# Issuing the stores of GpSimd-made rows two to four turns later, and the memory scan's transposes of h one turn later, in a two-layer attention and mixture-of-experts network on one core

## Chip, cores and metric

One NeuronCore of a Trainium2 chip (trn2) runs the whole program in one launch. The metric is the device time of one execution in microseconds (us). Before the change, three executions took 3901.26, 3905.21 and 3909.09 us; the median is 3905.21 us.

## What is computed

The input is x of shape 16 x 512 x 128 in fp32: 16 sequences of 512 tokens. Two layers follow each other, each with an attention part and a feed-forward part that read the same normalised input:

```python
x = L0_attn_x
xn = _layernorm(x, axis=-1)
x = x + _L0_attn_ref(xn, ...) + _L0_ffn_ref(xn, ...)
xn = _layernorm(x, axis=-1)
x = x + _L1_attn_ref(xn, ...) + _L1_ffn_ref(xn, ...)
```

- `_L0_attn_ref` is a small memory network, trained while it reads. The tokens are cut into 8 chunks of 64; for each chunk, in order, a two-layer perceptron (128 to 256 to 128, `h = silu(k @ w0.T)`, `y = h @ w1.T`, then an RMS norm) gets one clipped gradient step with momentum. This is the **scan**: 8 steps, each needs the weights that the step before it left. Afterwards every token is read through the final weights: the **readout**.
- `_L0_ffn_ref` is a convolution over time, full attention with 16 heads of 8, a layernorm, then 8 dense experts (128 to 512 to 128) weighted by a softmax gate, and a second layernorm.
- `_L1_attn_ref` is causal attention, a convolution of its context, a second causal attention with the convolved queries, and a projection.
- `_L1_ffn_ref` sends each token to its best 8 of 32 experts, with at most 128 tokens per expert.

## The kernel before, in words

**Turns.** The program is unrolled Python. Each piece of work on one sequence b is a generator that emits some instructions and then yields. A loop (`Turns.run`) steps every live generator once per *turn*: those with number 0 first (`tops`: scores and their row maxima), then 1 (`back`: scores again, exponentials, weighted values), then the rest. A stage is entered at a turn that is written into a table (`b * TA + 60` for `post0`, `t0 + b * TBB` for `middle`), or waits for a mark that another stage sets (`after`, `mark`). `idle(n)` yields n times and emits nothing.

**What a turn fixes.** TensorE's instructions run in exactly the order in which the turns emit them (`manual_schedule(engines=ORDERED)`, and ORDERED holds TensorE alone). On the other engines, and on SyncE's queue that issues nearly all transfers, a scheduler orders the instructions when the program is built; the place at which an instruction is emitted is its priority there. Once built, each queue is worked off strictly in its order: an instruction that waits for a semaphore holds up all that stand behind it.

**Filling.** A turn holds about 2.75 us of TensorE work by the kernel's own estimate (TURN). `ffn(b)`, the dense experts of layer 0, runs as a filler: per turn it emits as many of its 64 half-units as the credit left by the other stages allows. Where the turn has too little work for TensorE and no `ffn` work was emitted lately, `fill` adds one matmul whose result nobody reads.

**The stages, in order of time.** Turns 0 to 32 normalise x and load constants. From turn 32 to turn 486 the scan (8 steps, then 16 readouts, one begun every 6 turns) runs beside layer-0 attention (`front0`, `tops`, `back`, `post0`, one sequence each 32 turns) and `ffn`. From turn 480 on layer 1 follows at one sequence each 44 turns: `middle`, `front1`, `tops` and `back` for the first attention, `between`, `tops` and `back` for the second, `last`. Each of the 64 causal `tops` holds the lock "p1" for 11 turns, so 44 turns are exactly what four of them take. From turn 1165 the routed experts (`moe`) run beside the last three sequences; the last `last(15)` marks turn 1272, and the stages `total(b)` write the output.

**Stores of rows that GpSimd makes.** Four stages end a row of work on GpSimd and store it to device memory through SyncE:
- `post0(b)`, L1116: x1, after a layernorm whose last instruction is GpSimd's add at L237, to x1d. Then come four idle turns, then the transpose of x1 and its store at L1121, and the mark "x1", for which `ffn(b)` waits. x1d[0] is read back by `ffn` at L530 and, once `ffn` has rewritten it, by `middle` at L1163.
- `readout(b)`, L1034: y, after GpSimd's L1031 to L1033, to acc. It is the readout's last instruction. The tile y shares its buffer (tag h or ds, one buffer each) with the hTq of the readout two later.
- `middle(b)`, L1170: x2, after a layernorm and GpSimd's add at L1169, to acc. Then come three idle turns and the next layernorm.
- `last(b)`, L1279: x2, after GpSimd's add at L1278, to acc (for the 13 sequences that finish before the routed experts' counts are known).

Behind such a store on SyncE's queue stand, among others: the loads of the score operands kx and qx (L364), the little store of the row maxima and their two loads back (`top<-m` at L412, `qx<-top` at L416), the scan's token load xc (L778), and the experts' weights ew (L512, L516).

**The scan step.** `timed` starts each part at a turn counted from the step's start: `hidden(q)` for q = 0..3 at turns 1 to 4 (two pairs of matmuls into pp, two ACT instructions for the sigmoid sg, and one turn later VectorE's product h at L851 and three GpSimd instructions for the derivative ds at L853 to L855); `hidden_turned(q, i)` at turns 4 to 7 (four TensorE transposes of h, and the ACT copy to hT at L861); `gradient(0)` at 7 and `gradient(1)` at 9 (eight pairs of matmuls py from hT, then a chain over ACT, VectorE and GpSimd). The step goes on when all parts are through. `project(c + 2)` of the scan loads the tokens of a later chunk and makes its keys on GpSimd (L802 to L806).

Of the kernel before, what the change touches and what calls it, by code (L numbers as in the profile page):

```python
# [82 lines left out]
def network(ctx: ExitStack, tc: tile.TileContext, a, out):  # L83
# [85 lines left out]
    def drop():  # L169

        read[0] += 1
# [7 lines left out]
    def flat(ap):  # L179
        return ap.rearrange("p t d -> p (t d)")  # L180
# [84 lines left out]
    def idle(n):  # L265
        for _ in range(n):
            yield
# [494 lines left out]
    def scan(s1):  # L762
# [47 lines left out]
        def step(c):  # L810
# [47 lines left out]
            def hidden_turned(q, i):  # L858
                yield from room()
                tp = turn4(lambda t: h[:, 4 * q + t, i * P : (i + 1) * P])  # L860
                nc.scalar.copy(hT[q][:, i, :], tp)  # L861
                yield
# [49 lines left out]
            def back(q):  # L912
# [10 lines left out]
            yield from timed(  # L923
                (0, before()), (0, turned(kT, lambda t: k[:, t, :], 0)), (1, turned(kT, lambda t: k[:, 4 + t, :], 1)),
                *[(1 + q, hidden(q)) for q in range(4)],
                *[(4 + 2 * q + i, hidden_turned(q, i)) for q in range(2) for i in range(2)],
                (7, gradient(0)), (9, gradient(1)),
            )
            dyT = s1.tile([P, NT * P], F32, tag="kT", name="dyT")
            yield from timed(  # L930
# [58 lines left out]
        def readout(b):  # L989
            xb = s1.tile([P, TB, D], F32, tag=("k", "v")[b % 2], bufs=2, name="xb")  # L990
            nc.sync.dma_start(xb, x_b[b])
            xT = s1.tile([P, S], F32, tag=("hT0", "kT")[b % 2], name="xTr")
            nc.sync.dma_start(xT, xt[0, b])
            yield from idle(2)
            q = s1.tile([P, TB, D], F32, tag=("yh", "eb", "gy")[b % 3], name="rq")
            yield from silu_half(flat(q), lambda t: xT[:, t * P : (t + 1) * P], A("wq"))
            rq = sm.tile([P, TB], F32, tag="r_q", name="r_q")
            rms_rows(rq, q, TB, s1)
            nc.gpsimd.tensor_tensor(q, q, bc(row["qn"], 1, TB), ALU.mult)
            nc.gpsimd.tensor_tensor(q, q, bc(rq, 2, D), ALU.mult)  # L1000
            yield from idle(5)
            yield from room()
            qT = s1.tile([P, S], F32, tag="sg", bufs=2, name="qT")
            transpose_tokens(qT, q)
            yield from idle(1)
            hT = s1.tile([P, 2, S], F32, tag=("h", "ds")[b % 2], name="hTq")

            def hidden(i):
                yield from room()
                pp = hold("ppq")  # L1010
                mm(pp, w0T[:, i * P : (i + 1) * P], qT)
                nc.scalar.activation(hT[:, i, :], pp, AF.Tanh, scale=0.5)
                nc.scalar.activation(hT[:, i, :], hT[:, i, :], AF.Copy, scale=0.5, bias=0.5)
                yield
                nc.vector.tensor_tensor(hT[:, i, :], hT[:, i, :], pp, ALU.mult)
                drop()
                yield

            yield from side(hidden(0), hidden(1))
            yield from room()  # L1020
            py = toks(work("pyq"))
            for t in range(TB):
                for i in range(2):
                    mm(py[:, t, :], hT[:, i, t * P : (t + 1) * P], w1T[:, i, :], start=(i == 0), stop=(i == 1))
            ry = sm.tile([P, TB], F32, tag="r_yq", name="r_yq")
            y = s1.tile([P, TB, D], F32, tag=("h", "ds")[b % 2], name="yq")
            nc.scalar.copy(y, py)
            rms_rows(ry, y, TB, s1)
            yield from idle(3)
            nc.vector.tensor_tensor(y, y, bc(ry, 2, D), ALU.mult)  # L1030
            nc.gpsimd.tensor_tensor(y, y, bc(ln, 1, TB), ALU.mult)  # L1031
            nc.gpsimd.tensor_tensor(y, y, q, ALU.add)
            nc.gpsimd.tensor_tensor(y, y, xb, ALU.add)  # L1033
            nc.sync.dma_start(acc_b[b], y)  # L1034
            yield

# [58 lines left out]
    def post0(b):  # L1095
        yield from after(("back", 0, b, 0, 0), ("back", 0, b, 0, 1))
        z = live.pop((0, b))
        xcT, cn = z["xcT"], z["cn"]
        free_values.append(z["vp"])
        yield from room()  # L1100
        cT = fa.tile([P, S], F32, tag="st", bufs=2, name="cT")
        transpose_tokens(cT, cn)
        yield from idle(2)
        yield from room()
        po = toks(hold("po"))
        for t in range(TB):
            tk = slice(t * P, (t + 1) * P)
            mm(po[:, t, :], cT[:, tk], Wt("wo"), stop=False)
            mm(po[:, t, :], xcT[:, tk], ident, start=False)
        x1 = fa.tile([P, TB, D], F32, tag="x1", bufs=1, name="x1")  # L1110
        yield
        nc.vector.tensor_tensor(x1, po, bc(row["bo0"], 1, TB), ALU.add)
        drop()
        yield
        yield from layernorm(x1, x1, row["g1"], row["b1n"])
        nc.sync.dma_start(x1d[0, b], flat(x1))  # L1116
        yield from idle(4)
        yield from room()
        x1T = fa.tile([P, S], F32, tag="st", bufs=2, name="x1T")
        transpose_tokens(x1T, x1)  # L1120
        nc.sync.dma_start(x1d[1, b], x1T)  # L1121
        mark("x1", b)
        yield
# [35 lines left out]
    def middle(mid, b):  # L1159

        yield from after(("ffn", b))
        ac = mid.tile([P, TB, D], F32, tag="am", bufs=2, name="am")
        nc.sync.dma_start(flat(ac), x1d[0, b])  # L1163
        xa = mid.tile([P, TB, D], F32, tag="st", bufs=4, name="xa")
        nc.sync.dma_start(xa, acc_b[b])
        x2 = mid.tile([P, TB, D], F32, tag="st", bufs=4, name="x2")
        yield from idle(2)
        yield from layernorm(x2, ac, row["g2"], row["b2n"])
        nc.gpsimd.tensor_tensor(x2, x2, xa, ALU.add)  # L1169
        nc.sync.dma_start(acc_b[b], x2)  # L1170
        yield from idle(3)

        xwt = mid.tile([P, TB, XW], F32, tag="xwt", bufs=1, name="xwt")
        xn2 = xwt[:, :, 0:D]
        yield from layernorm(xn2, x2)
        yield from idle(3)
        yield from room()
        xT = mid.tile([P, S], F32, tag="st", bufs=4, name="xT2")
        transpose_tokens(xT, xn2)
        nc.sync.dma_start(xt[1, b], xT)  # L1180
        mark("x2", b)
        yield from idle(2)
        yield from room()
        prl = hold("prl")[:, 0 : TB * EXP1].rearrange("p (t e) -> p t e", e=EXP1)
        for t in range(TB):
            mm(prl[:, t, :], xT[:, t * P : (t + 1) * P], D1("gw"))
        yield
        lg = sm.tile([P, TB, EXP1], F32, tag="lg", name="lg")
        nc.vector.tensor_copy(lg, prl)
        drop()  # L1190
        t8 = sm.tile([P, TB, TOPK], F32, tag="t8", name="t8")
        lr = sm.tile([P, TB, EXP1], F32, tag="lr", name="lr")
        for t in range(TB):
            nc.vector.max(t8[:, t, :], lg[:, t, :])
            nc.vector.match_replace(lr[:, t, :], t8[:, t, :], lg[:, t, :], -BIG)
            if t == 1:
                yield
        yield
        nc.vector.tensor_tensor(lr, lr, lg, ALU.not_equal)
        nc.vector.tensor_tensor(lg, lg, bc(t8[:, :, 0], 2, EXP1), ALU.subtract)  # L1200
        yield
        nc.scalar.activation(lg, lg, AF.Exp)
        yield from room()
        pct = work("pct")[:, 0:P]
        mm(pct, lr.rearrange("p t e -> p (t e)"), row["tri"])
        ct = mid.tile([P, P], F32, tag="st", bufs=4, name="ct")
        nc.scalar.copy(ct, pct)
        for t in range(TB):
            of = ct[EXP1 * t : EXP1 * (t + 1), :]
            nc.sync.dma_start(ctab_v[:, b * TB + t, :], of)  # L1210
            nc.sync.dma_start(totT[:, b * TB + t : b * TB + t + 1], of[:, P - 1 : P])
        yield
        nc.vector.tensor_tensor(lg, lg, lr, ALU.mult)
        sw = sm.tile([P, TB], F32, tag="sw", name="sw")
        nc.vector.tensor_reduce(sw, lg, AX.X, ALU.add)
        nc.vector.reciprocal(sw, sw)
        nc.vector.tensor_tensor(xwt[:, :, D:], lg, bc(sw, 2, EXP1), ALU.mult)
        nc.sync.dma_start(xw_b[b], xwt)
        mark("xw", b)
        yield  # L1220
# [34 lines left out]
    def last(b):  # L1255
# [15 lines left out]
        if ("counted",) in done:  # L1271

            nc.sync.dma_start(ao[b], xo)
        else:
            x2 = l1.tile([P, TB, D], F32, tag="st", bufs=2, name="xs")
            nc.sync.dma_start(x2, acc_b[b])
            yield from idle(2)
            nc.gpsimd.tensor_tensor(x2, x2, xo, ALU.add)  # L1278
            nc.sync.dma_start(acc_b[b], x2)  # L1279
            whole.add(b)  # L1280
        mark("ao", b)
# [310 lines left out]
```

## Time and profile before

| | before |
|---|---|
| median of three runs | 3905.21 us |
| the profiled execution, whole | 3907.05 us |
| its span, first to last instruction | 3905.3 us |
| TensorE busy | 3452.3 us, 88% |
| VectorE busy | 2325.2 us, 60% |
| ScalarE busy | 2156.1 us, 55% |
| GpSimd busy | 1578.2 us, 40% |
| mean granted TensorE clock | 0.961 of full |
| DMA | 95 GB/s over the span |

The profile is that of one execution. In it L-numbers are lines of the kernel before; PE is TensorE's matmul, PEld its weight load, DVE VectorE, ACT ScalarE, POOL GpSimd, SPq SyncE's queue. `tile<-tile` names what an instruction writes and reads. A wait is put down to the semaphore that came last.

Since TensorE's order is the order of the turns, its instructions in the trace can be counted off against it, so each turn has a time. Turn 32 begins at 116 us, turn 486 at 1570 us, turn 1105 at 3418 us, turn 1165 at 3570 us and turn 1250 at 3849 us. So a turn takes 3.20 us in the scan's stretch, 2.99 us from there to turn 1105, 2.53 us where `ffn` is finished, 3.28 us beside the routed experts, and about 2 us at the very end.

### The profile page before, as it was taken

To read this page: it belongs to the slowest core of one execution; us is meant where nothing else is said; L and a number is where in the kernel's file an instruction comes from. 1 tells how busy PE (TensorE), PEld (TensorE's weight loads), DVE (VectorE), ACT (ScalarE), POOL (GpSimd) and SP (SyncE) were. 2 spreads that over 40 slices of the span, in tenths; PEclk is the share of its full clock that TensorE was granted. 3 is DMA by queue.
4 is the path that set the end of the run, shared out by engine and by line. 5 is a ranking of instruction groups with operands and counts; after the bars stand their busy time and mean duration, and the time that the engine had idled before them with its cause. 6 is when DMAs were issued, how large, how long until landed. Compare 5 with 4: busy or idle time off the path is not lost.

```text
span 3905.3 us, 61944 instructions
## 1 busy us (share of the span) xinstructions
PE 3452.3 (88%) x22265; PEld 1887.3 (48%) x22265; DVE 2325.2 (60%) x5027; ACT 2156.1 (55%) x3687; POOL 1578.2 (40%) x2522
## 2 busy tenths in 40 slices
PE   5999789889889899999998998899999999987877
PEld 2445445445444444555555555555555555533343
DVE  5666556565665555554565666566656666677762
ACT  1555555556566677665555565555555555543443
POOL 5432433344232555324244334433443344333664
PEclk7999899999999999999999999999999999997999
DMA  4222212222222233423443434343434434333343
GB/s 159 65 65 73 64 48 79 71 65 67 81 66 86 85 105 95 149 76 96 128 110 92 122 111 120 95 114 109 121 90 118 113 105 106 105 95 84 85 92 84
DMA packets 289940, 370.52 MB, mean 95 GB/s; under 512 B 46008, under 2 KB 141408, under 8 KB 289248
## 3 DMA queue, kind: packets, MB, share of 16 engines
q1 hardware_dynamic: 282464, 359.73, 32.1%
q0 software_dynamic: 7168, 6.82, 1.1%
q8 instruction: 177, 2.90, 0.3%
q14 instruction: 131, 1.07, 0.1%
HBM read 236.59 MB, written 133.25 MB: 95 GB/s over the span
## 4 chain that ended last, share of the span: by engine, by line
PE 67%; DVE 15%; POOL 6%; ACT 5%; issue 4%; DMA 3%; SPq 1%; POOLq 0%; ACTq 0%; DVEq 0%
PE s L192 17%; PE pye L591 12%; PE pc L192 11%; PE phe L192 11%; DVE nm L395 6%; DVE s L387 3%; PE tp L244 2%; DVE s L394 2%; PE pgr L192 2%; ACT e L466 2%; PE tpc L244 1%; PE pq L192 1%; PE pcv L192 1%; PE pj L192 1%; ACT sq L258 1%
## 5 line engine op out<-in xcount | busy, mean ns | idle before, releaser
L466 ACT ACTIVATE e<-s 128x1024 f32<-128x1024 f32 (+1 forms) x1216 | 1190.9, 979 | 697.0 <-PE s L192 616.6
L395 DVE TENSOR_REDUCE nm<-s 128x2 f32<-128x1024 f32 (+1 forms) x704 | 861.4, 1224 | 645.3 <-PE s L192 638.0
L387 DVE CUSTOM_DVE_ANT_0 s<-s,sb_const 128x512 f32<-128x512 f32 (+1 forms) x1024 | 646.7, 632 | 531.2 <-PE s L192 513.5
L470 POOL TENSOR_SCALAR_AFFINE_SELECT e<-e 128x128 f32<-128x128 f32 (+2 forms) x1408 | 468.8, 369 | 999.5 <-ACT e L466 997.2
L192 PE MATMUL s<-kx,qx 64*128 64x512 f32 (+3 forms) x3072 | 623.7, 432 | 274.3 <-DVE nm L395 145.1
L192 PEld LDWEIGHTS s<-kx,qx 64*128 64x128 f32 x3072 | 276.2, 188 | 913.1 <-issue 338.0
L192 PE MATMUL pc<-e,vp 128*32 128x512 f32 (+3 forms) x6144 | 658.9, 518 | 33.4 <-POOL e L470 33.2
L591 PEld LDWEIGHTS pye<-ew,hTe 128*128 128x128 f32 x4096 | 509.9, 193 | 148.1 <-issue 135.5
L581 ACT ACTIVATE hTe<-phe,sb_cols 128x512 f32<-128x512 f32 x512 | 354.0, 691 | 403.0 <-PE phe L192 401.2
L591 PE MATMUL pye<-ew,hTe 128*128 128x128 f32 x4096 | 575.5, 284 | 0.7 <-DVE vp L345 0.7
L192 PE MATMUL phe<-x1T,ew 128*128 128x512 f32 x1024 | 535.3, 607 | 3.2 <-DVE pr L545 1.0
L192 PE MATMUL s<-qx,kx 64*128 64x512 f32 (+3 forms) x3072 | 508.9, 356 | 31.5 <-ACT e L466 26.9
L192 PEld LDWEIGHTS s<-qx,kx 64*128 64x128 f32 x3072 | 288.1, 189 | 69.7 <-ACT e L466 56.0
L394 DVE TENSOR_TENSOR s<-s,sb_const 128x512 f32<-128x512 f32 (+1 forms) x192 | 168.4, 877 | 244.5 <-PE s L192 244.0
L599 POOL TENSOR_TENSOR ac<-ac,y 128x512 f32<-128x512 f32 x128 | 165.0, 1289 | 338.7 <-ACT y L598 337.9
L192 PEld LDWEIGHTS pc<-e,vp 128*32 128x32 f32 x6144 | 153.4, 111 | 275.9 <-issue 184.7
L598 ACT ACTIVATE y<-pye,pr 128x128 f32<-128x128 f32 x512 | 146.8, 368 | 40.7 <-PE pye L591 36.3
L192 PEld LDWEIGHTS phe<-x1T,ew 128*128 128x128 f32 x1024 | 158.9, 195 | 19.6 <-issue 10.4
L387 DVE DVE_READ_ACCUMULATOR2_ANT nm<- 128x1 f32 x1024 | 144.5, 141 | 0.0
L199 PE MATMUL fill<-sb_pb,sb_const 128*128 128x512 f32 (+2 forms) x236 | 118.4, 590 | 10.3 <-DMA sb_pb<-in_pb 10.2
L205 POOL TENSOR_SCALAR rs_t<-ss 128x4 f32<-128x4 f32 (+1 forms) x56 | 12.5, 223 | 245.5 <-ACT sq L258 244.5
L966 POOL TENSOR_TENSOR cl<-cl,phalf 128x1 f32<-128x1 f32 x8 | 4.5, 568 | 172.9 <-ACT cl L965 172.9
(291 smaller groups left out, 3885.5 us busy)
## 6 DMA issues: line engine op xcount, KB each, us to landing
ew<-in_ew SPq DMA_DIRECT2D x256, 256.0 KB
kx<-rk SPq DMA_DIRECT2D x192, 256.0 KB
qx<-rq SPq DMA_DIRECT2D x128, 256.0 KB
rq<-hi SPq DMA_DIRECT2D x64, 256.0 KB
rq<-lo SPq DMA_DIRECT2D x64, 256.0 KB
rk<-hi SPq DMA_DIRECT2D x64, 256.0 KB
rk<-lo SPq DMA_DIRECT2D x64, 256.0 KB
qx<-r SPq DMA_DIRECT2D x64, 256.0 KB
```

The lines of the kernel that those rows point to most:

```text
L192: nc.tensor.matmul(o, lhsT=lhsT, rhs=rhs, start=start, stop=stop)
L199: nc.tensor.matmul(o[:, 0:n], lhsT=ident, rhs=cell[0][:, 0:n], start=True, stop=True)
L244: nc.tensor.transpose(tp[:, t * P : (t + 1) * P], src(t), ident)
L387: newest[0] = nc.vector.tensor_tensor_reduce(out=sv[:, r, 0, :], in0=sv[:, r, 0, :], in1=row["caus"][:, S - n :], scale=1.0, scalar=-BIG, ...
L394: nc.vector.tensor_tensor(dg, dg, bc(bc(row["caus"][:, S - P :], 1, per), 1, 2), ALU.add)
L395: newest[0] = nc.vector.tensor_reduce(nm[:, qt, :, t : t + per], sv, AX.X, ALU.max)
L466: nc.scalar.activation(e[:, :, 0 : per * n], s[:, :, 0 : per * n], AF.Exp, scale=SCALE)
L470: cleared[0] = nc.gpsimd.affine_select(out=ev[:, r, :, 0:P], in_=ev[:, r, :, 0:P], pattern=[[0, per], [1, P]], compare_op=ALU.is_ge, fill= ...
L581: nc.scalar.activation(hs[i], ph, AF.Relu, bias=col("fb", i))
L591: nc.tensor.matmul(pye[0][:, t, :], lhsT=h[:, t * P : (t + 1) * P], rhs=w2[e][:, f, :], start=(f == 0 and t == 0), stop=(f == 3), skip_gro ...
L598: nc.scalar.mul(y[:, t, :], pye[0][:, t, :], pr[:, t, e : e + 1])
L599: nc.gpsimd.tensor_tensor(ac, ac, y, ALU.add)
```

## The change

The store in `post0` moves behind the four idle turns that stood after it; that in `middle` behind the three idle turns after it. The marks of these two stages come where they came. In `readout` three idle turns are put before the store and in `last` two; these two stages become that much longer. In the scan, the four `hidden_turned` parts and the two `gradient` parts start one turn later in each of the 8 steps. No instruction of the computation is added or taken away.

```diff
@@ scan, step(c)
-                *[(4 + 2 * q + i, hidden_turned(q, i)) for q in range(2) for i in range(2)],
-                (7, gradient(0)), (9, gradient(1)),
+                *[(5 + 2 * q + i, hidden_turned(q, i)) for q in range(2) for i in range(2)],
+                (8, gradient(0)), (10, gradient(1)),
@@ readout(b)
             nc.gpsimd.tensor_tensor(y, y, xb, ALU.add)
+            yield from idle(3)
             nc.sync.dma_start(acc_b[b], y)
@@ post0(b)
         yield from layernorm(x1, x1, row["g1"], row["b1n"])
+        yield from idle(4)
         nc.sync.dma_start(x1d[0, b], flat(x1))
-        yield from idle(4)
         yield from room()
@@ middle(b)
         nc.gpsimd.tensor_tensor(x2, x2, xa, ALU.add)
+        yield from idle(3)
         nc.sync.dma_start(acc_b[b], x2)
-        yield from idle(3)
@@ last(b)
             nc.gpsimd.tensor_tensor(x2, x2, xo, ALU.add)
+            yield from idle(2)
             nc.sync.dma_start(acc_b[b], x2)
```

## Prediction

> **What bounds the kernel now.** The page's busy line and its chain come first: TensorE is busy 88% of the span and carries two thirds of the chain; SyncE's queue carries 1%.
>
> ```profile
> PE 3452.3 (88%) x22265; PEld 1887.3 (48%) x22265; DVE 2325.2 (60%) x5027; ACT 2156.1 (55%) x3687; POOL 1578.2 (40%) x2522
> PE 67%; DVE 15%; POOL 6%; ACT 5%; issue 4%; DMA 3%; SPq 1%; POOLq 0%; ACTq 0%; DVEq 0%
> ```
>
> So the time is TensorE's work plus the stretches in which it stands, 3905.3 - 3452.3 = 453 us. The change removes no work; I ask which standing it removes and which it makes. Second, the waits of SyncE's queue: whom it waited for, total us, times, longest.
>
> ```profile
> SPq L412 <- ACT m L411: 543.7, 69, 31.1
> ...
> SPq L1034 <- POOL yq L1033: 146.6, 16, 15.6
> SPq L1170 <- POOL x L1169: 115.6, 13, 15.7
> SPq L1116 <- POOL x L237: 105.6, 11, 16.2
> ...
> SPq L1279 <- POOL xs L1278: 2.9, 2, 1.5
> ```
>
> Three of the four moved stores each block the queue for 100 to 150 us in all, the fourth for nothing. That is queue time, not kernel time: it counts only where TensorE ran out of something behind the store. So third, TensorE's own waits:
>
> ```profile
> PE s L192 <- DVE nm L395: 145.1, 141, 3.7
> ...
> PE s L192 <- DMA kx<-rk: 29.0, 6, 12.9
> ...
> PE tp L244 <- DVE h L851: 6.3, 4, 2.4
> ```
>
> Most standing is short and between TensorE and VectorE, which the change doesn't touch. Of the 29.0 us for kx, 11 lie at 49 to 52 us, before the first of these stores. The largest is 12.9; the timeline around it:
>
> ```profile
> 448.05 3.14 POOL L229 TENSOR_SCALAR x<-x,ln_mv,ln_rs 128x128 f32<-128x128 f32 x4
> 451.27 1.26 POOL L235 TENSOR_TENSOR x<-x,sb_rows 128x512 f32<-128x512 f32 x1
> 452.61 1.26 POOL L237 TENSOR_TENSOR x<-x,sb_rows 128x512 f32<-128x512 f32 x1
> ...
> 453.89 0.32 SPq L1116 DMA_DIRECT2D x1d<-x  x1
> 454.39 0.32 SPq L364 DMA_DIRECT2D kx<-rk  x1
> 454.76 1.27 SPq L416 DMA_DIRECT2D qx<-top  x2
> ...
> 457.55 0.76 PE L192 MATMUL s<-kx,qx 64*128 64x512 f32 x1 [12.93 <-DMA kx<-rk]
> ```
>
> GpSimd still had the scan's keys to make, so post0's layernorm ended at 453.87. The store had stood at the head of SyncE's queue since 440.0; kx and qx went out right behind it, and TensorE, which wanted kx at 444.6, stood 12.93 us and then 1.57 for the second kx load.
>
> **The change, part by part.** The sum is made against the profiled execution, 3907.05 us, 1.84 above the median of the runs.
>
> *Store of post0, four turns later.* In the changed program both kx loads, `top<-m` and both `qx<-top` of this place stand ahead of the store on SyncE. The last rk store was issued at 435.7 and such stores are seen to be waited for about 2 us, so kx can go at 440 and be there by 443, before TensorE asks at 444.6. Gain 12.93 + 1.57 = 14.5 us. Four turns of 3.2 us are 12.8, so the store now reaches the queue's head when GpSimd is about through.
>
> *The clock behind this stall.* The windows (us, then busy us and instructions of PE, PEld, DVE, ACT, POOL, then granted clock, DMA share, GB/s):
>
> ```profile
> 450.00:457.50 7.50, 0.00 (x0) 0.00 (x0) 0.00 (x0) 0.00 (x0) 5.93 (x6) 0.50 0.25 79
> 457.50:465.80 8.30, 6.68 (x20) 4.55 (x21) 2.42 (x3) 1.71 (x2) 1.05 (x1) 0.50 0.08 27
> ```
>
> TensorE works 8.3 us more at half clock. The same score matmul takes 0.76 us there and 0.50 at full clock, so of 6.68 us a third, 2.2, is lost. The Trainium skill (TensorE: Matmul & The Clock Gate, Part 1: The HAM clock gate) lets the clock come back after one busy window of about 3.4 us; by that rule only 3.4 x 6.68/8.3 / 3 = 0.9 us would be lost. I take the row: -2.2.
>
> *Other places where a moved store was seen ahead of a late load.* 1.62 us for xc at 804 (the store had blocked 9.7 us), and 1.11 + 0.29 for qx at 1714 behind the store at 1707.6. Gain 3.0; none or all of it may come. At the other waits above no TensorE instruction waited on what stood behind; `middle`'s 16 are worth nothing by the trace, so what stands behind them had cover.
>
> *A rule against it.* The Trainium skill (DMA: Bandwidth & Descriptors, Rules for kernel authors) advises to issue a DMA early and wait on its semaphore late. By it, later stores cost up to four turns, 13 us, each, where a reader is waiting. Here the early issue moves no byte earlier: the store sat 13.8 us at the head and went when GpSimd was done. Readers: `ffn` reads x1d[0] back right behind the store for sequence 0 alone and needs it some turns later; for the rest it is more than 30 turns later. Cost 0; with the cover gone, one 13 us for sequence 0. The readout's y tile is needed by the hTq two readouts on, 12 turns after its own, which leaves 3 turns behind the new store; and measured waits of 146.6/16 = 9.2 us put the store there already. 0. `last`'s store gains 2.9 at most and TensorE never waits for it: 0.
>
> *Transposes of h one turn later.* TensorE stood 6.3 us for h (four times, none over 2.4) and 1.2 for hT before py. h is late because ScalarE's sg waits 1.77 us for GpSimd's ds in these turns; a turn of 3.2 us covers that. Ends: -7.5, and 0 if the wait only moves on to the next instruction. I take -5.
>
> *More turns.* The scan gets 8 + 3 = 11 turns longer (it ends at 497 instead of 486). Their room is filled by `ffn`, which is only pulled about: layer-1 attention starts by a table, and its "p1" lock is taken without a hole. `ffn` ends at turn 1121 instead of 1105, still ahead of turn 1140, when the last `middle` starts. Work is conserved, so 0. If the cover were gone (`ffn` late), 11 turns of 3.2 = 35 us; I see no way to that. The planner emits 114 filling matmuls instead of 118 (one of 512, two of 256, one of 128 columns less, pairs at 1.05, 0.70 and 0.39 us): -2.8.
>
> *The end.* The planner's turns are 1278 instead of 1272. In the new order sequence 13 takes "p1" before sequence 15, so sequence 15's second attention starts 6 turns later: `tops` runs alone for 8 turns and `back` alone for 8, and after the routed experts 23 turns follow instead of 18. Price from above: 6 turns at the 2.05 us of the last stretch, 12.3. From below 0: the TensorE work of those turns is gone from the turns of 3.28 us beside the experts. Nearer to conservation, since these are waits on GpSimd's queue that lone turns have fewer of: +5.
>
> *Collisions dealt anew.* All steps of the scan, their token load xc and their keys on GpSimd with them, shift against post0's 32-turn beat. The stretch has other long stands on engine order (8.10 at 693, 5.69 at 1313, 3.90 at 959, 3.73 at 589, 3.30 at 868: 24.7). They will come elsewhere; half to 1.6 times as much gives -12 to +15. As the before had its one long DMA stall removed and no other is looked at, I put +5.
>
> Sum: -14.5 - 2.2 - 3.0 - 5 - 2.8 + 5 + 5 = -17.5: 3889.5 for an execution like the profiled one, **3888 us** for the median.
>
> **Rivals.**
> - *Given back at the end.* The stall goes, but the end costs its 12.3 in full and the wait for h only moves: 3888 + 7.3 + 5 = 3900. For it: a lone `back` turn is 2.05 us although it holds half the work. Against: the experts' turns get lighter.
> - *Another head of the queue (slower).* SyncE's order changes all over. Place: the scan's stretch. `top<-m` (L412) waits for ScalarE's copy 69 times, up to 31.1 us, and there are waits of 28.4 and 32.4 behind ScalarE's squares; no kx load that TensorE stood for was behind one after 100 us. If one does now, TensorE stands as it did at 444: 13.8 us of queue gave 14.5. Price up to 28.4: 3916. It decides once the new stand exceeds 17 us. For it: the old stall was such luck, in one of 16 stores. Against: loads are emitted three turns before their use.
> - *The change doesn't do what it says:* the build could keep the stores where they were. At the place of the stall it doesn't: 3904.
>
> **Chances.** Forecast 0.55 (its own range 3876 to 3899), given back at the end 0.19, another head 0.23, no effect 0.03. What a measurement here tells from no change is 0.2%, 7.8 us: faster is below 3897.4, slower above 3913.0. Of the forecast 0.53 is faster and 0.01 each side of that bound and beyond the slow one; of the second case 0.02 faster, 0.16 the same, 0.01 slower; of the third 0.02 the same, 0.21 slower; the fourth the same. Together faster 0.55, same 0.22, slower 0.23. The range 3870 to 3917 leaves out the ends of collisions and tail beyond these.
>
> **What would show it.** No stand of TensorE over 10 us between 440 and 460 and clock 1.0 there; SyncE's waits at these three stores down from 368 us to under 100; no DMA-ended wait of TensorE over 3 us after 100 us; the waits for h under 2 us; turns after turn 1250 at about 2 us, some 5 more of them after the experts' last. Wrong it would be with a new long stand whose releaser is a load, or if the stretch from turn 1165 on is more than 12 us longer.

## The result, and the profile after

| | before | after |
|---|---|---|
| median of four runs each | 3907.15 us | 3880.46 us |
| lowest to highest | 3901.26 to 3912.88 | 3877.74 to 3889.84 |
| ratio, 95% interval | | 0.9936 [0.9917, 0.9956] |
| the profiled execution, whole | 3907.05 us | 3889.84 us |
| its span | 3905.3 us | 3887.6 us |
| mean granted TensorE clock | 0.961 | 0.955 |

Beside the three runs of before that the prediction had stands one more. The kernel became 26.7 us faster, 0.64%, more than the 0.2% that can be told from no change. The profiled execution of after is the longest of its four, so its trace shows 17 us of the 27; e2 below has the same order of TensorE's work, and its trace is the fastest of its own five. In the timelines shown from here on, rows are picked out and those between them left out. A first reading by the lines of the prediction: the page's busy line, then the waits of SyncE's queue (us in all, times, longest).

```profile
PE 3472.2 (89%) x22257; PEld 1904.3 (49%) x22257; DVE 2317.0 (60%) x5027; ACT 2155.6 (55%) x3687; POOL 1571.9 (40%) x2522
```

```profile
SPq L412 <- ACT m L411: 679.8, 77, 31.7
SPq L1118 <- POOL x L237: 90.7, 11, 23.8
SPq L1035 <- POOL yq L1033: 79.4, 12, 14.5
SPq L1172 <- POOL x L1170: 42.1, 13, 5.0
```

TensorE's busy time rose by 20 us although it does no more work (it stood for less, 38 us over the span, but ran at a lower mean clock). The stores of `post0` (now L1118), `readout` (L1035) and `middle` (L1172) still hold the queue for 212 us here; and the queue's largest wait, `top<-m`, grew by 136 us while the kernel got faster. The page's chain of waits can't be set beside that of before: in the trace of after it breaks off after 1% of the span.

TensorE's own wait for kx:

```profile
PE s L192 <- DMA kx<-rk: 12.7, 4, 9.3
```

The waits for kx fell from 29.0 to 12.7 us, and the longest of them now is the one at 49 us, before any of these stores. The place of the old stall, in the timeline (start, duration, engine, line, operation):

```profile
426.43 0.80 SPq L364 DMA_DIRECT2D kx<-rk  x2
440.12 1.27 SPq L416 DMA_DIRECT2D qx<-top  x2
450.96 0.34 SPq L1118 DMA_DIRECT2D x1d<-x  x1
```

The store goes out at 450.96, behind both `qx<-top` and the kx loads ahead of them; the score matmul that stood before runs at 442.97 without a wait for kx. The windows of this place (us, then busy us and instructions of PE, PEld, DVE, ACT, POOL, granted clock, DMA share, GB/s):

```profile
450.00:457.50 7.50, 6.27 (x38) 3.05 (x38) 7.50 (x10) 4.82 (x9) 4.13 (x4) 1.00 0.69 183
457.50:465.80 8.30, 8.02 (x52) 4.45 (x56) 6.88 (x12) 7.00 (x15) 1.36 (x1) 1.00 0.41 93
```

Before, these two windows had TensorE at 0.00 and 6.68 us and the clock at 0.50. So at this place the trace shows what the forecast's first step said. Which edit brought it about, and where the rest came from, the page does not say.

### The profile page after: what moved, and what is told of

Its sections match the earlier page's. It is cut to its first block, busy times and chain, and to the rows that moved or that the text cites. A ratio compares the mean times of both kernels' runs of the same rounds, so it can differ in the third digit from the quotient of the medians.

```text
span 3887.6 us, 61858 instructions
## 1 busy us (share of the span) xinstructions
PE 3472.2 (89%) x22257; PEld 1904.3 (49%) x22257; DVE 2317.0 (60%) x5027; ACT 2155.6 (55%) x3687; POOL 1571.9 (40%) x2522
## 5 line engine op out<-in xcount | busy, mean ns | idle before, releaser
L192 PE MATMUL s<-qx,kx 64*128 64x512 f32 (+3 forms) x3072 | 516.9, 360 | 19.0 <-ACT e L466 12.9
L199 PE MATMUL fill<-sb_pb,sb_const 128*128 128x512 f32 (+2 forms) x228 | 118.5, 609 | 10.6 <-DMA zrow<-zero 10.1
```

The source lines that it names most:

```text
L192: nc.tensor.matmul(o, lhsT=lhsT, rhs=rhs, start=start, stop=stop)
L199: nc.tensor.matmul(o[:, 0:n], lhsT=ident, rhs=cell[0][:, 0:n], start=True, stop=True)
```

## The experiments

Every run is compared with runs of the kernel before on the same chip. The ratio is this run's time by that of before, so below 1 is faster; by it 0.001 is 3.9 us. "Standing" is time in which neither PE nor PEld works. Turns are counted off in each trace by TensorE's order, as in the prediction.

| run | edit to the kernel before | median us | ratio, 95% |
|---|---|---|---|
| e1_stores | the four stores, scan untouched | 3906.45 | 1.0001 [0.9991, 1.0010] |
| e2_scan | the scan's parts alone | 3881.11 | 0.9939 [0.9927, 0.9952] |
| e3_one_store | `post0`'s store of sequence 2 alone | 3907.61 | 1.0000 [0.9991, 1.0008] |
| e4_other_store | the same of sequence 4 alone | 3907.28 | 1.0001 [0.9991, 1.0010] |
| e5_store_behind_kx | sequence 2's store tied behind the kx load | 3897.60 | 0.9968 [0.9956, 0.9979] |
| e6_hidden_only | only the transposes of h a turn later | 3899.66 | 0.9978 [0.9967, 0.9989] |
| e7_gradient_only | only the gradients a turn later | 3884.92 | 0.9941 [0.9924, 0.9957] |
| e8_scan_and_end | e2, and sequence 15 before 13 at "p1" | 3871.81 | 0.9911 [0.9896, 0.9925] |
| e9_bare_turn | a bare turn in the middle of each scan step | 3910.04 | 1.0009 [1.0000, 1.0017] |
| e10_bare_turn_ahead | a bare turn at its head | 3835.01 | 0.9813 [0.9800, 0.9826] |
| e11_two_turns_and_end | transposes and gradients two turns later, and e8's end | 3924.08 | 1.0041 [1.0027, 1.0054] |
| e12_bare_turn_tied | e9, sequence 6's store tied behind kx | 3893.83 | 0.9973 [0.9963, 0.9984] |

### Which half of the change: e1, e2

e1 has the change's hunks in `readout`, `post0`, `middle` and `last`; e2 has only its first hunk, in the scan.

> The four stores moved, the scan's parts left where they were. TensorE's order is that of the kernel before (1272 turns, 118 fills), so nothing of the end changes. Theory A (one stall: the store of post0 for sequence 2 that held up kx, with its half-clock time): 17 to 20 us less than before, ratio 0.9955. Theory B (the scan's later transposes bring the gain): within 5 us of before. Theory C (the gain is collisions dealt anew by any edit): anything within 10 us of before.

> Only the scan's hidden_turned and gradient one turn later; all stores as before. 1278 turns, 114 fills. Theory A: -5 for the waits for h, -3 for the fills, +9 for the end (the two traces show the stretch from turn 1165 on 9 us longer), so within 5 us of before, unless the shift of one turn moves the sequence-2 collision by itself. Theory B: most of the 26.7 us of the change, 20 us or more less than before.

The stores are worth nothing and the scan's two lines are worth everything: 0.9939 against the 0.9936 of the whole change. e1 still shows the stall, and its SyncE waits behind `middle`'s store (now L1172) did fall, from 115.6 us to 9.6:

```profile
456.26 0.76 PE L192 MATMUL s<-kx,qx 64*128 64x512 f32 x1 [12.94 <-DMA kx<-rk]
```

```profile
SPq L1172 <- POOL x L1170: 9.6, 1, 9.6
```

The time did not move. So that wait was, as the prediction held, queue time without a reader behind it.

### One store alone: e3, e4

```diff
-        nc.sync.dma_start(x1d[0, b], flat(x1))
+        if b != 2:
+            nc.sync.dma_start(x1d[0, b], flat(x1))
         yield from idle(4)
+        if not (b != 2):
+            nc.sync.dma_start(x1d[0, b], flat(x1))
```

e4 has 4 in place of 2.

> The kernel before with post0's store four turns later for sequence 2 alone. Theory A: the stall of 14.5 us and its half-clock goes: 15 to 18 us less than before, nearly all that e1 brings. Theory B or many small waits: less than 5 us.

> The same edit for sequence 4 alone, a store that waited 7.5 us with no late load behind it. Theory A: 0, within 3 us of before, and the stall at 444 to 458 us stays. Theory C: as far from before as e3, several us either way, because any edit makes the scheduler order the queues anew.

Neither did anything, and the trace of e3 at the old place shows why:

```profile
453.01 0.32 SPq L1120 DMA_DIRECT2D x1d<-x  x1
453.50 0.32 SPq L364 DMA_DIRECT2D kx<-rk  x1
456.81 0.76 PE L192 MATMUL s<-kx,qx 64*128 64x512 f32 x1 [13.07 <-DMA kx<-rk]
```

The store, emitted four turns later in the source, still stands ahead of kx in the queue. In the builds of e3 and e4 the order of all 1946 transfers on SyncE is that of before; in e1, 14 of `post0`'s 16 stores kept their place. For these stores the place in the source, their priority for the scheduler, decided little; presumably it reckons with when the data are ready, which no run here shows. So e3 and e4 are two more measurements of the kernel before.

### The store really moved: e5

```diff
-                nc.sync.dma_start(
+                kload[0] = nc.sync.dma_start(
                     dst[64 * r : 64 * r + 32, :, :].bitcast(F32),
...
-        nc.sync.dma_start(x1d[0, b], flat(x1))
+        if not (b == 2):
+            nc.sync.dma_start(x1d[0, b], flat(x1))
         yield from idle(4)
+        if b == 2:
+            with tc.issue_after(kload[0].ins):
+                nc.sync.dma_start(x1d[0, b], flat(x1))
```

> The kernel before with post0's store of sequence 2 tied behind the kx load that had stood behind it; SyncE's order differs from before in these 12 places and in nothing else, all other engines' orders are the same. If the stall at 444 to 458 us is worth its own length on the path: 14 to 18 us less than before (ratio 0.9955 to 0.9965). If TensorE only stands elsewhere a little later (GpSimd is behind by the same work): under 5 us.

Here one store moves by 12 places and nothing else on any engine.

```profile
439.54 0.32 SPq L364 DMA_DIRECT2D kx<-rk  x1
445.82 0.50 PE L192 MATMUL s<-kx,qx 64*128 64x512 f32 x1 [1.43 <-DMA kx<-rk]
```

kx goes out at 439.54 instead of 454.39, TensorE stands 1.43 us, for the second kx load, instead of 12.93 and 1.57, and the time falls by 10.4 us of the medians (12.5 by the ratio, whose interval allows 8 to 17). From turn 118 to 160 the trace has 136.7 us instead of 149.5: 11.2 less standing and 1.6 less work time, the clock's share. This is the stall's price, by itself.

### Which of the scan's two lines: e6, e7

e6 has `5 + 2 * q + i` for the transposes and leaves 7 and 9 for the gradients; e7 has 8 and 10 for the gradients and leaves `4 + 2 * q + i`.

> Only the four hidden_turned parts one turn later, gradient where it was: 1272 turns, the scan ends at turn 486 as before, and the store of sequence 2 still stands ahead of kx. If the slack before the transposes of h is what counts: 5 to 9 us less than before. If it is the longer scan step and the new order of the queues: 0 to 5 us less, the stall at 444 stays.

> Only the two gradient parts one turn later: 1278 turns, the scan ends at turn 497, and kx now stands ahead of the store of sequence 2, all as in e2, but the transposes of h have no more slack than before. If the longer step and the new order bring the gain: 18 to 24 us less than before. If the slack for h does: less than 10 us.

The gradients' turn alone, which the title does not name, gives what both give (0.9941 and 0.9939), and in its trace TensorE waits no less for h (15.0 us against 14.3). It lengthens the scan (end at turn 497) and in its build the scheduler puts kx ahead of the store. With the transposes alone the scan ends at 486 as before and the store stays ahead; its gain of 0.2% is 8.6 us. Its trace is of its slowest execution, 3908.92 us, and so can't show the whole of it: TensorE's waits for h are 10.1 us there instead of 14.3, and standing in the scan's stretch is 143.8 us against 146.0. With both lines, where TensorE waited for h, the wait moved on: before, 6.3 us for the transposes and 8.0 at three instructions behind them (pjk 3.9, ptp 2.4, tpm 1.7); after, 0.9 and 13.2 (pj 4.8, pjk 3.7, phe 2.9, tpm 1.8).

### The end: e8

```diff
         early = 0 if b < B - 1 else 12 if i else 16 + 8 * c
+        if (b, i, c) == (B - 3, 1, 1):
+            early = -20
```

With e2's two lines. Sequence 13 asks for "p1" 20 turns later, so that sequence 15 takes it first, as in the kernel before.

> e2 with the last second-attention of sequence 13 held back by 20 turns, so that sequence 15 takes the lock in time: 1271 turns instead of 1278. If the two lone streams at the end cost what the two traces show from turn 1165 on: 6 to 10 us less than e2, about 3873. If TensorE's work is conserved there: within 3 us of e2.

The last 335 us of the program, from turn 1165, in the windows of before, after and e8:

```profile
3569.90:3905.25 335.35, 257.86 (x1628) 125.46 (x1628) 186.44 (x513) 124.16 (x175) 190.72 (x302) 0.93 0.37 89
```

```profile
3542.90:3887.60 344.70, 273.86 (x1578) 132.35 (x1578) 182.22 (x504) 120.20 (x171) 185.97 (x295) 0.86 0.36 85
```

```profile
3525.00:3860.00 335.00, 253.07 (x1570) 122.70 (x1567) 182.36 (x503) 120.06 (x169) 186.63 (x294) 0.91 0.38 90
```

After is 9 us longer than before. It does not stand more (60.2 us against 67.3, up to TensorE's last instruction); it does fewer matmuls in more busy time, with the granted clock at 0.86 instead of 0.93. With sequence 15 in time the end is back at 335 us. Those with TensorE's old order (before, e1, e3, e4, e5) have 333 to 338 us here and clocks of 0.897 to 0.925; after, e2 and e7 have 343 to 345 and 0.858 to 0.869. By the ratios of e8 and e2 the end is worth 11 us, give or take 7; their traces differ by 8 here. It is not the only thing that moves this stretch: e9, e11 and e12 below, with sequence 15 in time, take 340 to 342 us, as much as e10 without it.

The part of it ahead of turn 1261, beside the routed experts, in before and after:

```profile
3569.90:3872.90 303.00, 239.86 (x1534) 117.06 (x1534) 184.97 (x510) 119.10 (x169) 183.55 (x291) 0.93 0.37 85
3543.30:3850.70 307.40, 247.60 (x1420) 120.77 (x1420) 179.66 (x498) 108.91 (x156) 175.02 (x270) 0.85 0.35 80
```

After has 114 matmuls fewer there and takes no less time (the five with the old order take 302 to 308 us). Behind turn 1261 stand the turns that were added: 37 us in after, e2 and e7, and 30 to 32 in the five and in e8.

### Is it the longer scan step? e9, e10, e11

After e8 these terms had been measured: 12 for the stall, 11 lost at the end, nothing for the stores. That leaves some 25 us of gain. In the scan's stretch (turn 86 to the scan's end) e2 has 108.0 us of standing where the four traces with the old order (before, e1, e3, e4) have 146 to 150, and its stands over 3 us sum to 11 us instead of 38. Two readings were open: a longer step gives the engines slack, or the new alignment of steps and attention happens to be a good one. e9 adds one `yield` behind the updates of each step, e10 one at its head:

```diff
             gy = late["gy"]
+            yield
             yield from room()
```

```diff
+            yield
             yield from timed(
                 (0, before()), (0, turned(kT, lambda t: k[:, t, :], 0)), (1, turned(kT, lambda t: k[:, 4 + t, :], 1)),
```

> Before, with one bare turn in each scan step, ahead of the projections of the gradients (behind the updates of the step): no transpose is moved, but the scan ends at turn 496 instead of 486, and in the build kx stands ahead of the store of sequence 2. Theory A (a longer scan step by itself thins out what stands on the engines' order): as in the run with the scan's edit alone, standing of TensorE in the scan's stretch 108 to 116 us instead of 146, about -50 us at turn 1165, ratio 0.993 to 0.995. Theory B (beyond the stall, the gain comes from moving the gradients behind the transposes, not from the length): only the stall's 12 us, standing about 134, ratio 0.996 to 0.998. Theory C (alignment by luck): anything from 0.994 to 1.002, with new long stands in other places.

> Before, with one bare turn at the head of each scan step: all parts of the step keep their spacing, the scan ends at turn 498 instead of 486, and in the build kx stands ahead of the store of sequence 2. Theory A (length by itself): ratio 0.993 to 0.995 and standing 108 to 116 us in the scan's stretch. Theory B (spacing inside the step): 0.996 to 0.998, standing about 134. Theory C (alignment by luck): this and the other bare turn differ from each other by more than 0.3%.

> The transposes of h and the gradients two turns later instead of one, and sequence 15 given its lock in time; the scan ends at turn 505. If slack for h and its gradients is what pays, the ratio is at or below the 0.991 of the run with one turn and the same end, and the waits for h, below 1 us, are gone. If the gain of the one turn was its alignment, it is 0.992 to 1.0, with stands over 3 us back at 20 us or more in the scan's stretch.

All three lengthen the scan (to turn 496, 498 and 505), and they lie 2.3% apart: 3910, 3835 and 3924 us. Slack as such is refuted by e9 and e11. That the gain comes from the gradients' new place behind the transposes (theory B) is not needed: e10 moves no part against another within the step and has 105.3 us of standing in the scan's stretch, as little as e2; and e11, which moves the gradients further, loses. What remains is alignment, with effects larger than the change that is studied. This is reached by exclusion; no run moves the alignment alone and holds the rest, and for e2's own gain theory B is not excluded. e9 kept kx ahead of sequence 2's store, and lost the gain at another store:

```profile
854.70 0.50 SPq L412 DMA_DIRECT2D top<-m  x1
871.74 0.32 SPq L1117 DMA_DIRECT2D x1d<-x  x1
872.23 0.32 SPq L364 DMA_DIRECT2D kx<-rk  x1
875.42 0.79 PE L192 MATMUL s<-kx,qx 64*128 64x512 f32 x1 [13.83 <-DMA kx<-rk]
```

It is the old stall at sequence 6: the queue's head waits 16.5 us for GpSimd's L237, kx stands behind, TensorE stands 13.8 us. This is what the prediction's rival "another head of the queue" described, with a store in place of `top<-m` at the head, and in a kernel that was not the one predicted.

e10's gain over e2 does not come from the scan: at turn 600 they are 63 us (e10) and 73 us (e2) ahead of before. The windows of turns 600 to 1105, e2 first, then e10:

```profile
1836.00:3368.00 1532.00, 1390.70 (x9970) 811.65 (x9970) 935.28 (x2446) 855.16 (x1348) 595.04 (x1281) 0.96 0.37 107
```

```profile
1845.00:3332.00 1487.00, 1373.35 (x9984) 803.52 (x9982) 937.27 (x2446) 856.78 (x1356) 594.99 (x1279) 0.99 0.39 110
```

The same amount of work, 45 us less. 17 of it is TensorE's busy time, with the clock at 0.99 instead of 0.96; 27 is standing (111 us against 138), spread over many stands none of which exceeds 3 us. e11 has 147 us there, some 20 of it at `phe`, put down to VectorE's `lo` (L326), a wait that is not among those of e2 and e10. Why e10's order fits this stretch so well is open.

### The queue's head once more: e12

e12 is e9 with e5's tie, for sequence 6. In SyncE's queue only this store moves.

> The bare turn behind the updates again, with one edit more: the store of sequence 6 is tied behind the second kx load, as that of sequence 2 was. In the build only this store moves in SyncE's queue, from ahead of the two kx and the two qx loads to behind them; TensorE's order stays. Theory Q (the head of SyncE's queue is what made this variant lose the gain): kx goes out right behind top<-m at 855 us instead of 872, the stand of 13.8 us at 862 and the half clock behind it are gone, 12 to 17 us less than the bare turn alone, 3893 to 3898, ratio about 0.9965 to before. Theory R (the rest of the scan's stretch takes it back): the same 3910 within 5 us, with a new stand over 3 us within the next 100 us.

```profile
855.94 0.50 SPq L412 DMA_DIRECT2D top<-m  x1
857.65 0.32 SPq L364 DMA_DIRECT2D kx<-rk  x1
863.82 0.50 PE L192 MATMUL s<-kx,qx 64*128 64x512 f32 x1 [0.57 <-DMA kx<-rk]
```

It takes 14 us less than e9 by the two ratios (16 by the medians, which come from different chips), as theory Q had it. From turn 246 to 278 the trace has 102.2 us instead of 118.1; standing fell by 13.5 and the rest by 2.4, with the clock at 1.00 instead of 0.93. And with both its stalls gone, e12 lies where e5 lies (0.9973 and 0.9968): this bare turn brings nothing beyond the stall.

## Why the prediction was right, and where not

The forecast, 17.5 us off 3907.05, had the sign and lay 8 us from the measured median. It was right with a wrong cause at its head, without a term of its own for the gradients' turn that brought the gain (only its length and "collisions"), and with two terms whose errors partly cancel. That it came so near was luck.

- *The stall at 444 us:* the mechanism held, and three quarters of the size. Forecast -14.5 and -2.2 for the clock; measured alone, -12.5 in time (e5) and -11.2 of standing and -1.6 of work time in the trace; at the sister place in e12 -14 in time, -13.5 and -2.4 in the trace. Of the 14.5 us, 1.4 stayed as a stand for the second kx load, and 1.9 came back in short stands of the next turns. For the clock the prediction took the row and not its working by the rule of the Trainium skill (TensorE: Matmul & The Clock Gate, Part 1: The HAM clock gate), one busy window of about 3.4 us: 1.6 and 2.4 lie about the row's 2.2, above the estimate of 0.9 so worked out. The rule itself is not refuted by this, since it asks for at least one sustained window: TensorE stood once more until 459.88, and full clock was back 5.9 us later.
- ***Failed:* "Store of post0, four turns later".** The prediction saw the loads ahead of the store in the build of the whole change and put that down to the store's edit. The built orders of single parts show that the scan's gradients did it; the store's edit left the store where it was (e1, e3). The rival "the change doesn't do what it says" got a chance of 0.03, because it was judged at the place of the stall and from the whole build. For 14 of `post0`'s 16 stores it was true. That later stores cost nothing held (e1, 1.0001).
- *SyncE's waits at three stores, 368 us to under 100:* 212 us in the rows above. The stores moved less than the source says, and `middle`'s wait vanished in e1 without any effect on the time, which bears out the reasoning that these waits cost nothing.
- *The small late loads, -3.0:* did not come in sum. After 100 us, TensorE's waits that a DMA ended, without the stall, are 9.7 us before and 11.3 after; none of after's is over 3 us, as the prediction said.
- *Transposes of h, -5:* open. Alone they gave 8.6 us (e6, interval 4 to 13), with 14.3 us of such waits down to 10.1. In the change as a whole the lower bound, "0 if the wait only moves on", is nearer: 14.3 became 14.1, and with the gradients already moved, moving the transposes too changed 0.9941 to 0.9939.
- *"8 + 3 = 11 turns":* the three did not come from the readout. With the stores alone the scan ends at 486; all 11 come from the scan's parts. That `ffn` would cover them held: it ended in time.
- *Fills, 114 instead of 118:* the trace has 114.
- *The end, +5:* mis-sized. It measured 8 to 9 us in the traces and 11 by e8, inside the bounds of 0 to 12.3. Conservation of work was the wrong guide, for a reason that it leaves out: ahead of turn 1261, 114 fewer matmuls took no less time, at a clock of 0.85 instead of 0.93, so nothing came back there for the 5 to 7 us that the added turns cost behind it. Both parts of the rival "given back at the end" happened, this one and the wait for h that only moves; its 3900 us was missed for the term that follows.
- *Collisions dealt anew, +5:* mis-sized and of the wrong sign. What is left of 26.7 after the stall and the end is about -25 (-22 if the fills brought their 2.8), outside the -12 to +15 that were allowed. For edits of a line or two this term ranges from nothing (e12 beside e5) to some -60 us (e10: -73 in all, 12 of it the stall) and to some +28 (e11: the stall gone, yet 16 us slower). The bounds had been taken from the stands over 3 us alone. Those did fall, without the stall from 24.7 us in the scan's stretch to 11.3 in e2 and 14.4 in after, close to the lower bound. But the shorter stands fell too, by 11 us over the span of e2 and by 31 over that of e10, and the time in which TensorE works moved by +8 and -11 us.

So the stall's removal was certain once the built order was known, and the rest of this change's gain looks like one draw from a wide distribution. e10 is faster than after by 1.2%, and e8 by 0.2%, within the noise; neither was derived from a rule that would have told it beforehand.

## What to carry to other kernels

Where a scheduler orders a queue, read the built order of each part of a change by itself before putting an order down to a line of the source; if a transfer must stand behind another, tie it there. A queue's wait counts only by what is due behind it: 13.8 and 16.5 us at the head cost 12.5 and 14 us of kernel where a score operand stood behind, and over 100 us of waits cost nothing where none did. In a kernel of many interleaved stages, an edit that shifts one of them can re-align the rest, here with -1.9% to +0.4%, so an expected gain of under 1% needs a run that isolates it, and a bare shift is a fair control.

## What was not expected of the hardware

The clock follows the stands late: a stand of 13 us was followed by half clock until 8.3 us (before) and 6.4 us (e9) after TensorE had work again. In the last stretch, where after stands 7 us less than before, it still took 9 us longer with the granted clock at 0.86 instead of 0.93: there 1578 matmuls took 273.86 us, and 1628 took 257.86 before. e2 and e7, with the same end, have 0.869 both.

A long stand is not needed for this. In the trace of after, half clock set in 50 times between 100 us and the last 5 us of TensorE's work; 43 times no stand of over 3 us lay in the 6.8 us ahead of it. At 3646.7 us the longest was 2.2 us, in a stretch in which TensorE worked 1.20 of 3.40 us, and half clock lasted 17.1 us:

```profile
3643.30:3646.70 3.40, 1.20 (x18) 0.60 (x18) 0.35 (x2) 1.50 (x2) 0.54 (x2) 1.00 0.91 176
3646.70:3663.80 17.10, 12.76 (x56) 5.91 (x56) 11.71 (x27) 4.80 (x7) 4.74 (x11) 0.50 0.03 7
```

Short stands cost clock as well, so the sum of the long ones does not tell the price.
